# Batch 0's latent attention in one written order of instructions

## The chip, the cores and the metric

The kernel runs on one core of a Trainium2 chip. A core has five engines with a queue each: TensorE (PE) multiplies matrices and writes its products to PSUM, VectorE (DVE) works on vectors, ScalarE (ACT) computes functions such as the exponential and copies, GpSimd (POOL) does vector work on SBUF, and SyncE (SP) starts transfers. Each engine takes its instructions in the order of its own queue and waits, where it must, on semaphores of the others. The metric is the time of one execution on the device in microseconds (us), lower is better. The kernel before took 2269.19 us, the median of three runs between 2260.75 and 2271.79.

## The reference, cut to what matters

Two layers work on x, 2 batches of 1024 tokens with 128 features. Each step adds its result to x. The change is in the first step alone, a causal attention with 16 heads of 64 whose keys and values come from a latent of 32 numbers per token:

```python
q_blhd = jnp.einsum('bld,dhk->blhk', x_bld, Wq)
latent_bll = jnp.einsum('bld,dc->blc', x_bld, Wkv_down)
k_blhd = jnp.einsum('blc,chk->blhk', latent_bll, Wk_up)
v_blhd = jnp.einsum('blc,chk->blhk', latent_bll, Wv_up)
attn = jnp.einsum('bqhd,bkhd->bhqk', q_blhd, k_blhd) / jnp.sqrt(jnp.asarray(HD, dtype=x_bld.dtype))
...
attn = jax.nn.softmax(jnp.where(mask, attn, neg_inf), axis=-1)
...
x = x + _L0_attn_a_ref(_layernorm(x, axis=-1), L0_attn_a_Wq, L0_attn_a_Wkv_down, L0_attn_a_Wk_up, L0_attn_a_Wv_up, L0_attn_a_Wout)
x = x + _L0_ffn_ref(_layernorm(x, axis=-1), L0_ffn_W_fc, L0_ffn_W_proj)
x = x + _L0_attn_b_ref(_layernorm(x, axis=-1), ...)
```

After it come a feed-forward step with spiking counts, a state-space step (`attn_b`), the spiking step again, and a second layer with a linear attention, eight experts, an attention of 16 heads, and the experts again.

## The kernel before, in words

`LatentAttention` holds the first step. Wq and Wk_up are multiplied together beforehand (`wc`, scaled by 1/8), so that a head's queries live in the latent's 32 dimensions; Wv_up and Wout are multiplied to `wvo`. Tokens stand in 16 tiles of 128, four tiles make a chunk of 512, two chunks a batch. The 16 heads are C = 4 groups (`c`) of J = 4 (`j`); the four heads of a group lie in four quarters of 32 partitions.

1. `__init__` (line 135) builds constants on DVE: the mask, and the selections `ones`, `pick` and `addm`, 16 small steps of three instructions (lines 161 to 163).
2. `project` (line 168) loads five weights on ACT's queue, forms `wc` and `wvo` (16 small products each, lines 186 and 194), and then, for each of the four chunks: norm (bn_stats and bn_aggr, a square root on ACT, an inverse and four normalising instructions on DVE), four transposes, the latents in two layouts (`latT`, `lat`), and the queries of the four groups (line 221). PSUM tiles are copied out by DVE and ACT. The norm's square root and the softmax's exponential are in different function tables of ACT.
3. `row_maxima` (line 227) finds each query's largest score, exactly, before any exponential. For each tile `i` of 128 queries, each group `c` and each stretch of up to 512 keys it makes the scores of four heads on PE (line 243, with a mask product at line 252 on the last stretch) and DVE reduces them (line 261). Batch 0 takes all four heads to one PSUM tile of four banks, with two such tiles; batch 1 takes two heads to a tile of two banks, with three tiles. At the end DVE splits the negative maxima into three bf16 terms (line 272), PE transposes these and DVE copies them to `nmT`.
4. `attend` (line 283) has units (half of the queries, group, tile of 128 keys): 4 x 4 for the first half of 512 queries and 4 x 8 for the second. A unit is: scores with keys on the partitions (line 330), the maxima subtracted by a product with `addm` (line 339), the exponential on ACT (line 353), on a diagonal tile a mask on POOL (line 356), and two steps later the product with the latents (`weigh`, line 389). Denominators are, with `added`, sums over the key tiles on DVE (line 401) and one product per group (line 372); without it, one product per unit. `end` (line 407) closes a half. A unit's two PSUM tiles come from a pool of three (`a0_st`, two banks each); the outputs `a0_oT` and denominators `a0_dT` have the last two banks.

Batch 0's projections and maxima are put into order by the compiler's planner, which may move instructions ahead of others; the products are in `manual_schedule`, where every engine keeps the order in which the program writes its instructions. The helper `weave(main, side, rate)` runs `rate` steps of `side` after each step of `main`, `alternate` takes turns, `follow` puts streams one after the other, and `drain` runs a stream to its end. `first_layer` (line 1314) calls it all: project for both batches, batch 0's maxima, batch 0's products, and then, in `manual_schedule` too, the later steps of batch 0 with batch 1's maxima (rate 1.1) and products woven between them.

Of the kernel before, what the change touches and what calls it, by code (L numbers as in the profile page):

```python
# [1 line left out]

# [7 lines left out]
F32 = mybir.dt.float32  # L10
# [95 lines left out]
def drain(steps):  # L106
    for _ in steps:
        pass
# [20 lines left out]
class LatentAttention:  # L129
# [5 lines left out]
    def __init__(self, g, w, keep):  # L135
# [15 lines left out]
        nc.vector.memset(self.ones, 0.0)  # L151

        self.pick = keep.tile([P, C, P], F32, name="a0_pick")
        nc.vector.memset(self.pick, 0.0)
        for c in range(C):
            nc.vector.memset(self.ones[:, c, c::C], 1.0)
            for j in range(J):
# [8 lines left out]
                )  # L166

    def project(self, pools):
# [6 lines left out]
        with g.tc.tile_pool(name="a0_prep", bufs=1) as prep, g.tc.tile_pool(name="a0_pp", bufs=6, space=PSUM) as pp:  # L175
            w = {}
            for name in ("wkd", "wqT", "wkupT", "wvupT", "wout"):
                w[name] = g.load(name, g.dram[name], list(g.dram[name].shape), nc.scalar, prep)
            wc = prep.tile([P, 16 * LD], F32, name="a0_wc")
            wk4 = prep.tile([P, J, LD], F32, name="a0_wk4")  # L180
            for j in range(J):
                nc.gpsimd.tensor_copy(wk4[:, j, :], w["wkd"])

            psw = pp.tile([P, 512], F32, name="a0_ps")
            for h in range(16):
                nc.tensor.matmul(
                    psw[:, h * LD : (h + 1) * LD], w["wqT"][:, h, :], w["wkupT"][:, h, :], start=True, stop=True
                )

            nc.scalar.mul(wc, psw, 0.125)  # L190
            psv = pp.tile([P, C, D], F32, name="a0_ps")
            for h in range(16):
                c, j = divmod(h, J)
                nc.tensor.matmul(
                    psv[32 * j : 32 * j + 32, c, :], w["wvupT"][:, h, :], w["wout"][:, h, :], start=True, stop=True
                )
            nc.vector.tensor_copy(self.wvo, psv)

            for n in range(4):
                b, m = divmod(n, 2)  # L200
                cols = bass.ts(m, 512)
                u = prep.tile([P, 4, D], F32, name="a0_u", bufs=2)
                uT = prep.tile([P, 512], F32, name="a0_uT", bufs=2)
                ln = StagedNorm(g, g.x[:, 4 * n : 4 * n + 4, :], 4, "a0")
                ln.stats(range(4))
                ln.root()
                ln.inverse()
                ln.apply(u, range(4), nc.vector)
                pt = pp.tile([P, 4, P], F32, name="a0_ps")
                transpose4(g, pt, u)  # L210
                nc.vector.tensor_copy(uT, pt.rearrange("p a b -> p (a b)"))
                pl = pp.tile([P, 512], F32, name="a0_ps")
                nc.tensor.matmul(pl, wk4.rearrange("p a b -> p (a b)"), uT, start=True, stop=True)
                nc.scalar.copy(self.latT[b][:, cols], pl)
                plt = pp.tile([P, 4, LD], F32, name="a0_ps")
                for t in range(4):
                    nc.tensor.matmul(plt[:, t, :], uT[:, bass.ts(t, P)], w["wkd"], start=True, stop=True)
                nc.vector.tensor_copy(self.lat[b][:, 4 * m : 4 * m + 4, :], plt)
                for c in range(C):
                    pq = pp.tile([P, 512], F32, name="a0_ps")  # L220
                    nc.tensor.matmul(pq, wc[:, bass.ts(c, P)], uT, start=True, stop=True)
                    if c % 2:
                        nc.scalar.copy(self.qT[b][:, c, cols], pq)
                    else:
                        nc.vector.tensor_copy(self.qT[b][:, c, cols], pq)

    def row_maxima(self, b, seq, ps, together):


        nc, C, J = self.g.nc, self.C, self.J  # L230
        qT, latT = self.qT[b], self.latT[b]

        nm = seq.tile([P, 2, TPB, C * J], F32, name="a0_nm")
        for i in range(TPB):
            nk = (i + 1) * P
            for c in range(C):
                for half, n0 in enumerate(range(0, nk, 512)):
                    n = min(nk - n0, 512)
                    last = n0 + n == nk
                    ss = [ps.tile([P, together, 512], F32, name="a0_s", tag="a0_s") for _ in range(J // together)]  # L240
                    for j in range(J):
                        quad = slice(32 * j, 32 * j + 32)
                        nc.tensor.matmul(  # L243
                            ss[j // together][:, j % together, :n],
                            qT[quad, c, bass.ts(i, P)],
                            latT[quad, n0 : n0 + n],
                            start=True,
                            stop=not last,
                        )
                    if last:  # L250
                        for j in range(J):
                            nc.tensor.matmul(  # L252
                                ss[j // together][:, j % together, n - P : n],
# [5 lines left out]
                    for k, s in enumerate(ss):  # L259
                        h = c * J + k * together  # L260
                        nc.vector.tensor_reduce(  # L261
                            nm[:, half, i, h : h + together], s[:, :, :n], AX.X, ALU.max, negate=True
                        )
                    yield
        two = TPB // 2
        nc.vector.tensor_tensor(nm[:, 0, two:, :], nm[:, 0, two:, :], nm[:, 1, two:, :], ALU.min)
# [1252 lines left out]
```

## Time and profile before

| | |
|---|---|
| median of 3 runs | 2269.19 us |
| the profiled execution's own time | 2268.1 us |
| its span | 2266.4 us |
| PE busy over the span | 1974.6 us (87%) |
| DVE busy | 1694.8 us (75%) |
| ACT busy | 1188.3 us (52%) |
| POOL busy | 908.5 us (40%) |
| first maximum of batch 0 on DVE | 50.98 us |
| first exponential of batch 0 on ACT | 146.42 us |
| last instruction of batch 0's products on DVE | 282.8 us |

The profile is of one execution. Busy times are sums over an engine's instructions; matmuls are pipelined, so that a busy PE need not be at its peak. PE's granted clock is given as a share of full speed. In a group's line stand the source line, the engine, the operation, output and input tiles with shapes, the count, the busy time with the mean in ns, and after the second bar the idle time just before these instructions with what ended it. In a list in order of time stand start and length in us, and in square brackets the idle time before and what ended it. Tile names are cut: `a_nm` is `a0_nm`.

### The profile page before, as it was taken

The page shows a single profiled execution, that of the slowest core. Times are in us where ns is not written, and L with a number is a line of the kernel's source. Part 1 is how long each engine was busy: PE and PEld are TensorE (multiplying, and loading weights), DVE is VectorE, ACT ScalarE, POOL GpSimd, SP SyncE. Part 2 cuts the span into 40 slices and gives each one's busy share as a digit, 9 for nine tenths or more (in the row PEclk, how much of TensorE's full clock was granted, in tenths as well). Part 3 has the DMA queues.
Part 4 walks back from the last instruction along what each step waited for, and adds up shares of the span by engine and source line. Part 5 has one row for each costly group of instructions (what it writes and reads, how often), then busy time and mean ns, then how long its engine had stood idle before and what let it go on. Part 6 is the DMA issues. An engine that isn't in the chain of part 4 may idle for free. (4 is left out here: it accounts for less than half of the span.)

```text
span 2266.4 us, 36372 instructions
## 1 busy us (share of the span) xinstructions
PE 1974.6 (87%) x14832; PEld 1157.8 (51%) x14832; DVE 1694.8 (75%) x2054; ACT 1188.3 (52%) x1497; POOL 908.5 (40%) x480
## 2 busy tenths in 40 slices
PE   7679888779967558899898798988999999999999
PEld 4223343223334123344446576766777777777753
DVE  5966767897856789945323898988898899998822
ACT  1026512366624637734223675756777777777722
POOL 0013300063401020100101578887787777787720
PEclk9889988889988769999999899999999999999999
DMA  3000000395730577500000455565555555555500
GB/s 88 1 1 1 1 1 6 88 224 142 174 112 10 138 186 167 131 0 0 1 0 1 121 150 154 151 162 139 160 150 154 149 150 152 156 153 143 153 11 5
DMA packets 73798, 220.15 MB, mean 97 GB/s; under 512 B 9184, under 2 KB 19872, under 8 KB 73504
## 3 DMA queue, kind: packets, MB, share of 16 engines
q1 hardware_dynamic: 54736, 149.40, 22.0%
q0 software_dynamic: 18432, 67.12, 15.1%
q8 instruction: 116, 1.90, 0.4%
q10 hardware_dynamic: 464, 1.33, 0.3%
q14 instruction: 50, 0.41, 0.1%
HBM read 78.35 MB, written 5.24 MB: 37 GB/s over the span
## 5 line engine op out<-in xcount | busy, mean ns | idle before, releaser
L1193 POOL TENSOR_TENSOR h_a<-h_e,h_r 128x2048 f32<-128x2048 f32 x128 | 583.0, 4555 | 140.6 <-PE h_po L1199 100.2
L1159 DVE TENSOR_REDUCE h_m<-h_s 128x128 f32<-128x2048 f32 x128 | 293.2, 2291 | 70.9 <-PE h_s L1148 70.9
L1183 PE MATMUL h_pd<-h_e,ident 128*128 128x128 f32 x2048 | 264.7, 283 | 37.9 <-DMA h_e<-h_e 24.6
L1165 DVE TENSOR_TENSOR h_e<-h_s,h_m 128x2048 f32<-128x2048 f32 x128 | 292.4, 2284 | 2.3 <-DVE h_m L1159 0.6
L1168 ACT ACTIVATE h_e<-h_e 128x1024 f32<-128x1024 f32 x256 | 256.6, 1049 | 66.8 <-DVE h_e L1165 60.7
L1183 PEld LDWEIGHTS h_pd<-h_e,ident 128*128 128x128 f32 x2048 | 242.4, 194 | 80.6 <-DVE x_res L1032 47.6
L1004 ACT ACT_TABLE_LOAD x110 | 141.1, 1283 | 162.2 <-PE e_pgu L997 162.0
L356 POOL TENSOR_SCALAR_AFFINE_SELECT a_pT<-a_pT 128x256 f32<-128x256 f32 x120 | 125.9, 1072 | 223.3 <-ACT a_pT L353 137.5
L917 DVE TENSOR_TENSOR e_h<-e_sg,e_pu 128x512 f32<-128x512 f32 x128 | 87.0, 684 | 162.1 <-PE e_pu L910 136.4
L261 DVE TENSOR_REDUCE a_nm<-a_s 128x2 f32<-128x1024 f32 (+7 forms) x144 | 168.1, 1217 | 39.1 <-PE a_s L252 24.2
L912 ACT ACTIVATE e_sg<-e_pg 128x512 f32<-128x512 f32 x128 | 76.1, 596 | 191.1 <-PE e_pg L909 172.6
L1023 PEld LDWEIGHTS h_pd<-Wd,e_h 128*128 128x128 f32 x1024 | 125.1, 191 | 95.1 <-DVE e_h L1012 78.1
L353 ACT ACTIVATE a_pT<-a_st 128x1024 f32<-128x1024 f32 (+3 forms) x176 | 129.9, 792 | 72.8 <-PE a_st L339 72.0
L746 DVE TENSOR_TENSOR_SCAN s_h<-s_a,s_h 128x1024 f32<-128x1024 f32 x64 | 149.0, 2328 | 20.1 <-ACT s_a L714 15.4
L1148 PE MATMUL h_s<-h_qz,h_kT 32*128 32x512 f32 x1024 | 148.9, 651 | 17.1 <-DVE h_e L1165 12.1
L997 PE MATMUL e_pgu<-e_uT,Wg 128*128 128x256 f32 x512 | 155.0, 385 | 2.6 <-ACT h_qz L1112 2.1
L910 PE MATMUL e_pu<-e_uT,Wu 128*128 128x512 f32 x256 | 139.1, 626 | 19.5 <-DVE e_h L917 19.5
L1023 PE MATMUL h_pd<-Wd,e_h 128*128 128x128 f32 x1024 | 149.7, 288 | 6.6 <-DVE e_h L1012 3.6
L1178 POOL DMA_DIRECT2D h_e<-h_e x128 | 114.9, 898 | 100.8 <-DVE h_m L1159 48.7
L243 PE MATMUL a_s<-a_latT,a_qT 32*128 32x512 f32 (+3 forms) x768 | 117.7, 590 | 41.3 <-DVE a_nm L261 39.2
L997 PE MATMUL e_pgu<-e_uT,Wu 128*128 128x256 f32 x512 | 153.2, 381 | 0.0
L1168 ACT ACT_TABLE_LOAD x111 | 142.4, 1283 | 12.0 <-issue 7.7
(268 smaller groups left out, 3235.8 us busy)
## 6 DMA issues: line engine op xcount, KB each, us to landing
h_e<-h_e SPq DMA_DIRECT2D x128, 512.0 KB, 3.8
h_e<-h_e POOLq DMA_DIRECT2D x128, 512.0 KB, 4.5
s_a<-s_steps SPq DMA_DIRECT2D x64, 512.0 KB, 4.9
s_h<-s_steps SPq DMA_DIRECT2D x64, 512.0 KB, 6.4
s_steps<-s_gate SPq DMA_DIRECT2D x8, 256.0 KB, 3.6
Wg<-in_Wg_dram SPq DMA_DIRECT2D x8, 256.0 KB, 6.0
Wu<-in_Wu_dram SPq DMA_DIRECT2D x8, 256.0 KB, 5.9
Wd<-in_Wd_dram SPq DMA_DIRECT2D x8, 256.0 KB, 6.1
```

Of the source, the lines that this page charges most:

```text
L261: nc.vector.tensor_reduce(nm[:, half, i, h : h + together], s[:, :, :n], AX.X, ALU.max, negate=True)
L746: nc.vector.tensor_tensor_scan(h, a, h, 0.0, ALU.mult, ALU.add)
L910: nc.tensor.matmul(pu, w["Wu"][:, e, f], opened[n], start=True, stop=True)
L997: nc.tensor.matmul(pgu[:, k, :], w[name][:, e, f], uT, start=True, stop=True)
L1004: nc.scalar.activation(sg, pgu[:, 0, :], AF.Silu)
L1023: nc.tensor.matmul(po[:, t, :], h[:, bass.ts(t, P)], self.w["Wd"][:, e, fc, :], start=(k == 0), stop=(k == 1))
L1148: nc.tensor.matmul(s[:, j, :].rearrange("p (k q) -> p k q", k=K), kTs[b][quad, bass.ts(kb, P)], qzs[b][quad, :, bass.ts(qb, P)], start=Tru ...
L1159: nc.vector.tensor_reduce(m, heads.rearrange("p h q -> p q h"), AX.X, ALU.max)
L1165: nc.vector.tensor_sub(e, heads, m.unsqueeze(1).to_broadcast([P, H, P]))
L1168: nc.scalar.activation(eh, eh, AF.Exp, scale=scale)
L1183: nc.tensor.matmul(pd, g.ident, e2[:, k, :], start=(k == 0), stop=(k == 7))
L1193: nc.gpsimd.tensor_mul(a, e, r.unsqueeze(1).to_broadcast([P, H, P]))
```

## The change

Everything of batch 0's first step, the projections of both batches included, now stands in one `manual_schedule`. The methods become generators whose pieces are interleaved by hand, and one pool of three PSUM tiles of two banks (`a0_st`) serves projections, maxima and products of batch 0. Projections are made chunk by chunk; chunk 0 comes first, in turns with the query weights. Maxima are made by halves of the queries, with two heads to a PSUM tile in both batches, and each half's maxima are split and transposed on their own. The first half's maxima are woven with chunk 1 and the selections (0.6 steps to a unit); then come chunk 2 and the value weights; then the first half's products with the second half's maxima and chunk 3 (2.7 steps to a unit), and last the second half's products. The first half's denominators are now one product per unit (`added=(False, True)`). The large fills of `ones` and `pick` go to POOL, and all PSUM copies of the projections and of `nmT` to ACT.

```diff
-        nc.vector.memset(self.ones, 0.0)
...
-        nc.vector.memset(self.pick, 0.0)
+
+    def selections(self):
...
+        nc.gpsimd.memset(self.ones, 0.0)
+        nc.gpsimd.memset(self.pick, 0.0)
         for c in range(C):
...
+            yield
+
+    def open(self, pools, prep):
...
+    def query_weights(self, ps):
+        nc, w, LD = self.g.nc, self.pw, self.LD
+        psw = ps.tile([P, 2, 512], F32, name="a0_st")[:, 0, :]
+        for h in range(16):
+            nc.tensor.matmul(
+                psw[:, h * LD : (h + 1) * LD], w["wqT"][:, h, :], w["wkupT"][:, h, :], start=True, stop=True
+            )
+            if h == 7:
+                yield
+
+        nc.scalar.mul(self.wc, psw, 0.125)
+        yield
+
+    def value_weights(self, ps):
...
+        nc.scalar.copy(self.wvo, psv)
+        yield
+
+    def project(self, n, ps):
...
+        two = lambda: ps.tile([P, 2, 512], F32, name="a0_st")
...
+        ln.stats(range(4))
+        ln.root()
+        yield
+        ln.inverse()
+        ln.apply(u, range(4), nc.vector)
+        yield
+        pt = two()
+        transpose4(g, pt[:, 0, :].rearrange("p (a b) -> p a b", a=4), u)
+        nc.scalar.copy(uT, pt[:, 0, :])
+        yield
+        pl = two()
+        nc.tensor.matmul(pl[:, 0, :], self.wk4.rearrange("p a b -> p (a b)"), uT, start=True, stop=True)
+        nc.scalar.copy(self.latT[b][:, cols], pl[:, 0, :])
+        for t in range(4):
+            nc.tensor.matmul(pl[:, 1, bass.ts(t, LD)], uT[:, bass.ts(t, P)], w["wkd"], start=True, stop=True)
+        nc.scalar.copy(
+            self.lat[b][:, 4 * m : 4 * m + 4, :], pl[:, 1, 0 : 4 * LD].rearrange("p (a b) -> p a b", a=4)
+        )
+        yield
+        for c in range(0, C, 2):
+            pq = two()
+            for k in range(2):
+                nc.tensor.matmul(pq[:, k, :], self.wc[:, bass.ts(c + k, P)], uT, start=True, stop=True)
+            nc.scalar.copy(self.qT[b][:, c : c + 2, cols], pq)
+            yield
+
+    def row_maxima(self, b, half, seq, ps, tag):
...
+        nm = seq.tile([P, 2, T, C * J], F32, name="a0_nm")
+        terms = seq.tile([P, T, P], BF16, name="a0_terms")
+        nc.gpsimd.memset(terms, 0.0)
+        for i in range(T * half, T * half + T):
...
-                    ss = [ps.tile([P, together, 512], F32, name="a0_s", tag="a0_s") for _ in range(J // together)]
+                    ss = [ps.tile([P, 2, 512], F32, name=tag) for _ in range(J // 2)]
...
-        nc.vector.tensor_copy(self.nmT[b], pt.rearrange("p a b -> p (a b)"))
-        yield
...
+        nc.scalar.copy(self.nmT[b][:, bass.ts(half, 512)], pt.rearrange("p a b -> p (a b)"))
+        yield
...
-        latent.project([pool(es, "a0_batch0", 1), own])
-        with tc.tile_pool(name="a0_seq", bufs=1) as seq, tc.tile_pool(name="a0_ps_a", bufs=2, space=PSUM) as ps:
-            drain(latent.row_maxima(0, seq, ps, 4))
-        work = pool(es, "a0_work", 2)
+        latent.open([pool(es, "a0_batch0", 1), own], pool(es, "a0_prep", 1))
+        seq, work = pool(es, "a0_seq", 1), pool(es, "a0_work", 2)
         ps, ps_o = pool(es, "a0_ps_b", 3, space=PSUM), pool(es, "a0_ps_o", 1, space=PSUM)
-        with tc.manual_schedule(engines=ALL):
-            drain(latent.attend(0, work, ps, ps_o, added=True))
+        drain(alternate(latent.project(0, ps), follow(iter([None]), latent.query_weights(ps))))
+        maxima = [latent.row_maxima(0, half, seq, ps, "a0_st") for half in range(2)]
+        side = follow(latent.project(1, ps), latent.selections(), latent.project(2, ps), latent.value_weights(ps))
+        weave(islice(maxima[0], 16), side, 0.6)
+        next(maxima[0])
+        drain(islice(side, 4))
+        drain(maxima[0])
+        drain(side)
+        attend = latent.attend(0, work, ps, ps_o, added=(False, True))
+        side = follow(maxima[1], latent.project(3, ps))
+        weave(islice(attend, 15), side, 2.7)
+        drain(side)
+        drain(attend)
...
-            maxima = latent.row_maxima(1, aseq, ps, 2)
+            maxima = follow(*[latent.row_maxima(1, half, aseq, ps, "a0_s") for half in range(2)])
```

## The prediction

> **What bounds the kernel now.** I read the page first, then the busy time by stretch of the first 443 us, then groups with shapes kept apart, then the instructions in order of time around the places where the new order cuts in. The page says that the change touches little: the chain that ended last lies in the second layer, and the slices show TensorE (PE) at 6 to 9 tenths in the first fifth of the span, where this change is. So the answer comes from that fifth. In stretches (the columns are length, then busy us and instructions of PE, its weight loads, VectorE = DVE, ScalarE = ACT, GpSimd = POOL, then PE's granted clock):
>
> ```profile
> 0.00:29.00 29.00, 18.33 (x86) 13.57 (x87) 20.36 (x110) 4.13 (x8) 1.81 (x12) 1.00 0.75 172
> 29.00:50.00 21.00, 17.97 (x71) 9.54 (x69) 8.25 (x17) 5.85 (x10) 0.52 (x1) 1.00 0.00 0
> 50.00:78.00 28.00, 21.42 (x216) 10.25 (x220) 25.73 (x18) 0.00 (x0) 0.43 (x1) 0.95 0.01 1
> 78.00:142.50 64.50, 37.93 (x308) 15.16 (x300) 58.14 (x37) 0.00 (x0) 0.00 (x0) 0.87 0.00 1
> 142.50:181.20 38.70, 35.66 (x312) 13.23 (x312) 13.16 (x19) 22.56 (x34) 13.86 (x30) 0.81 0.01 1
> 181.20:283.00 101.80, 93.81 (x803) 35.37 (x801) 76.30 (x82) 60.14 (x80) 37.54 (x36) 0.98 0.01 1
> ```
>
> These are weights and chunk 0 of the projections (0 to 29), chunks 1 to 3 (to 50), maxima of the first half of batch 0's queries (to 78), of the second half (to 142.5), products of the first half up to its last unit (to 181.2), and the rest of the products. To see: DVE carries the maxima (84 of 92 us), PE the products (129 of 140) and most of the projections. Two long stretches with different bounds stand in series, which is the room that the change aims at. But DVE is busy 20 us in the first 29, where PE waits for weights until 9.75, so some of its work is already covered there.
>
> The prices of a maximum, four heads to an instruction now (first two lines), two heads in batch 1, which the changed batch 0 will use too (last four):
>
> ```profile
> L261 DVE TENSOR_REDUCE a_nm<-a_s 128x4 f32<-128x2048 f32 x24 | 53.9, 2283 | 5.1 <-PE a_s L243 4.6
> L261 DVE TENSOR_REDUCE a_nm<-a_s 128x4 f32<-128x1536 f32 x8 | 13.8, 1750 | 0.3 <-PE a_s L252 0.2
> ...
> L261 DVE TENSOR_REDUCE a_nm<-a_s 128x2 f32<-128x1024 f32 x48 | 56.4, 1217 | 14.1 <-PE a_s L243 9.4 <-PE a_s L252 4.5
> L261 DVE TENSOR_REDUCE a_nm<-a_s 128x2 f32<-128x768 f32 x16 | 14.5, 948 | 4.1 <-PE a_s L252 4.0
> L261 DVE TENSOR_REDUCE a_nm<-a_s 128x2 f32<-128x512 f32 x16 | 10.3, 685 | 7.9 <-PE a_s L252 7.9
> L261 DVE TENSOR_REDUCE a_nm<-a_s 128x2 f32<-128x256 f32 x16 | 6.0, 414 | 5.0 <-PE a_s L252 5.0
> ```
>
> And how three PSUM tiles of two heads behave in batch 1, in order of time:
>
> ```profile
> 428.01 1.13 PE L243 MATMUL a_s<-a_latT,a_qT 32*128 32x512 f32 x4
> 428.21 2.35 DVE L261 TENSOR_REDUCE a_nm<-a_s 128x2 f32<-128x1024 f32 x2
> 429.49 1.13 PE L243 MATMUL a_s<-a_latT,a_qT 32*128 32x512 f32 x4 [0.35 <-DVE a_nm L261]
> 430.55 0.40 PE L252 MATMUL a_s<-a_mask,a_identb 128*128 128x128 bf16 x4
> 430.87 2.36 DVE L261 TENSOR_REDUCE a_nm<-a_s 128x2 f32<-128x1024 f32 x2 [0.31 <-PE a_s L252]
> ```
>
> To see: where the second tile of a unit waits for a buffer, its two pairs of heads take 1.13 us each, against 1.14 for all four together in an undisturbed unit; and DVE stands 0.31 us per masked unit. PE goes on only as far as the rotation of three tiles lets it.
>
> **The change part by part.** I follow the new order stage by stage and compare when it reaches the last unit of the first half's products, at 181.2 now.
>
> Chunk 0. PE starts at 9.75 as now, since the five weight loads keep their place on ACT's queue and the loads on SP's are not moved. At the cold prices of now: query weights 7.0, transposes 1.1, latents 2.05 + 1.75, queries 5.3: done at 27, first maximum at 28, instead of 51. Selections and value weights have left this stretch, and so have chunks 1 to 3.
>
> First half's maxima with chunk 1 and three quarters of the selections. DVE: 8 x (0.414 + 0.685 + 0.948 + 1.217) = 26.1; chunk 1's norm 3.1 (four each of 0.285, 0.159 and 0.28, and an inverse); the selections cost 8.4 now (16 x 0.215, 0.171, 0.141), so 6.3. Sum 35.5. Selections were hidden under the weights' arrival; that cover is gone, and behind them in DVE's queue stand maxima, for which PE's tiles wait. Gaps: 0.31 x 16 less the five places that inserted DVE work fills, 3.4; chunk 1's insertions on PE (transposes 0.6, latents 2.1, two query pairs 1.84 each) with the next unit's 1.0 to 1.4, less the 1 to 2 us of maxima that DVE has in hand, open about 4. Together 43: to 71.
>
> Between the halves the order is serial. On DVE: three-term split 1.4, last selections 2.1, chunk 2's statistics 1.8, the root's round trip 0.5, inverse and normalising 1.3: 7.1. Only then PE's transposes of chunk 2, queued ahead of everything else, can go: PE stands 7 us. Then chunk 2 on PE and value weights with DVE empty. Chunk 0 took 18.5 to 29.2 cold, so 10.7; a warm chunk took 35.8 to 42.0, so 6.2; with maxima's transposes and value weights 13 cold, 8 warm. What a stop does to the clock is here:
>
> ```profile
> 135.00:141.00 6.00, 0.90 (x11) 0.50 (x8) 5.34 (x8) 0.00 (x0) 0.00 (x0) 0.62 0.00 1
> 141.00:147.00 6.00, 4.55 (x24) 1.86 (x21) 0.69 (x1) 1.86 (x2) 0.00 (x0) 0.50 0.00 0
> 147.00:153.00 6.00, 5.06 (x28) 1.97 (x28) 0.00 (x0) 3.96 (x6) 2.44 (x6) 0.50 0.00 0
> 153.00:159.00 6.00, 6.00 (x52) 2.19 (x50) 4.11 (x6) 2.04 (x4) 1.96 (x3) 0.67 0.01 3
> ```
>
> Five us without work cost the clock until about 158, so I take 13: 71 + 7 + 13 = 91 for the first product. [...]
>
> First half's products with the second half's maxima. DVE has 32 x 1.217 + 26.1 = 65 us over 32 units, woven 2.7 to a product step, so 12 steps of 5.4. What decides is how long DVE is empty per step. Take PE at the end of a step's last maximum: DVE has that unit's two tiles before it, on average 2.0 us. PE then writes the step's scores: the first pair at once (0.7 on average over widths 512, 384, 256, 128), the second when the first of the two tiles is reduced (1.1 to 1.8), bias terms 0.3 to 2.1. Behind these in PE's queue stand weighing and, since this half no longer sums on DVE, denominators: both have the rows 1.07, 0.85, 0.64, 0.42, mean 0.745, so 1.5, to 3.6. Next unit's scores 1.1: DVE gets work at 4.65, having been empty 2.65. Step: 5.4 + 2.65 = 8.05, twelve steps 97, to 188. Bounds: empty 0 (65, if PE always runs ahead) and 3.15 with 0.5 more for masks (103).
>
> Last three steps: split 1.4, three products of 3.7, 2.9 and 2.2 on PE, a warm chunk 3 of 6.2, and about 2 us in which PE waits for the norm, with its root between exponentials: 17.5, to 205.5. That root needs two ACT_TABLE_LOADs that are not there now, 1283 ns each by the page's row, 2.6 together, inside those 2 us. [...]
>
> The rest is the order of now, 101.8 us: end at 307.3 against 283.0, **+24**. Rest of the edits: copies moved from DVE to ACT (0.66 to 0.69 each, queries at 1.03 for 1024 columns) cost nothing where ACT is busy under a quarter; behind the products, 22.6 of 38.7, they add at most 2. POOL's fills (about 1 us) stand behind nothing. DVE's sums that go (13 us) lie beside PE. Batch 1's maxima in halves add five short operations of 0.25 and take a 0.69 copy to ACT, and halve the 4.2 us tail at 438.6: between -2 and +2, taken as 0. Profiled run 2268.1 (span 2266.4), 1 us under the median 2269.19: **2292**; its own range, stages at their bounds, 2276 to 2303.
>
> **The rivals.** (1) Not slower: DVE's empty time per step in the woven stretch goes. For: PE busy there is only 3.6 + 2.7 x 1.1 = 6.6 of 8.05. Against: one order per engine, three tiles. Fully gone it is worth 12 x 2.65 = 32: 2260; with a warm chunk 2 and no gaps in the first stretch 15 less. It decides from 0.65 us down, where 2.0 x 12 equals the 24. Chance 0.17 (2245 to 2274). (2) The clock falls at the stop and stays down for 17 us, as from 141 to 158, into the products: half of about 15 us, and again whenever PE starves: 2304 or more. For: the rows above. Against: PE is busier than that in the woven stretch. 0.14. (3) The change moves nothing on balance: front as fast as now (78) and the gaps half as long: 2268 less 0 to plus 10. 0.09. (4) Forecast as worked out, 0.60.
>
> **How the numbers follow.** Half a percent (11 us) is about what can be told from no change. Slower: most of the forecast's 0.60 (0.56) and rival 2, 0.70. Same: forecast's low end 0.04, rival 3, and 0.06 of rival 1, 0.19. Faster: 0.11, rival 1's rest. Range: 2257 leaves out 0.10 below, 2307 0.10 above.
>
> **What would show it.** First maximum near 28; a PE stop of 5 to 8 us near 71 to 78 with the clock at 0.5 behind it; first exponential near 91; in the woven stretch a period of about 8 us with DVE empty 2 to 3 us under "PE a_st"; its last unit near 205. Wrong if that period is 6 us or less, or if the first exponential comes before 80.

## The result, and the profile after

The kernel with the change took **2306.51 us** (median of four runs, 2304.51 to 2308.63) against 2270.49 us before (four runs, 2260.75 to 2272.13): 1.0161 times as long, with a 95% interval of 1.0141 to 1.018. The direction was forecast, the size was not: +36 us where +24 was predicted. The time lies above the 2276 to 2303 that the forecast gave as its own range.

The profiled execution took 2305.7 us (span 2304.0). The whole loss lies in batch 0's first step: its last addition to x (the DVE line `x_res<-x_res,a_st`) starts at 318.20 us, before at 282.07, so 36.1 later, and what follows lasts nearly as long as before (1985.8 us from there to the end of the span, against 1984.3). In this text "the end of the step" is always that instruction. It is a cleaner measure than the total, because the remaining 1980 us vary from one profile to the next, between 1979 and 1996 in the runs below.

Busy time by stretch of the kernel after, cut where the stages of the prediction meet (columns: length, then busy us and count of PE, its weight loads, DVE, ACT, POOL, then PE's granted clock, DMA share, GB/s):

```profile
0.00:28.00 28.00, 18.72 (x66) 12.81 (x66) 3.40 (x17) 5.29 (x8) 3.27 (x16) 1.00 0.78 177
28.00:76.90 48.90, 41.02 (x204) 19.26 (x202) 32.86 (x85) 4.11 (x7) 0.00 (x0) 0.69 0.00 1
76.90:96.00 19.10, 12.12 (x50) 6.31 (x54) 5.72 (x31) 3.73 (x7) 0.00 (x0) 0.54 0.00 0
96.00:201.20 105.20, 94.72 (x656) 38.09 (x644) 61.65 (x65) 18.92 (x29) 10.08 (x25) 0.85 0.00 1
201.20:217.40 16.20, 13.12 (x101) 5.74 (x98) 4.22 (x19) 10.72 (x15) 2.48 (x6) 1.00 0.00 1
217.40:318.90 101.50, 94.26 (x813) 36.05 (x812) 73.73 (x76) 60.92 (x81) 38.42 (x36) 0.97 0.01 1
```

The first row is chunk 0, and DVE is busy for 3.4 us of it where it had 20.4 of its first 29 before: the cover that the selections had is empty now. The second row is the first half's maxima. The clock, third from the end of each row, is what the prediction did not have: 0.69, 0.54 and 0.85 in three stretches in a row, where the same work before ran at 1.00 (projections) and 0.87 to 0.95 (maxima). PE is busy for 41.0 of the 48.9 us of the second row, which holds chunk 1 too; with four heads to a tile and no chunk beside them it was 21.4 of 28.0. One reading of the clock is not to be trusted: the first row says 1.00, but chunk 0's first latent product takes 2.07 us there, and the same product 1.13 us in the kernel before at 30.48 us, so chunk 0 ran cold now as it did before.

Within the second row the clock is low twice before PE stops, and PE is busy both times:

```profile
33.00:48.00 15.00, 14.32 (x70) 8.30 (x67) 6.79 (x15) 1.44 (x3) 0.00 (x0) 0.50 0.00 1
64.00:73.00 9.00, 8.66 (x28) 2.95 (x28) 7.08 (x18) 0.00 (x0) 0.00 (x0) 0.50 0.00 0
```

The stop between the halves, PE in order of time (start, length, instructions, and in brackets the idle time before and its releaser):

```profile
72.05 0.61 PE L276 MATMUL a_st<-a_mask,a_identb 128*128 128x128 bf16 x4
82.89 1.15 PE L115 MATMUL a_st<-ident,a_u 128*128 128x128 f32 x4 [10.24 <-DVE a_u L74]
...
89.26 6.21 PE L245 MATMUL a_st<-a_uT,a_wc 128*128 128x512 f32 x8
95.39 1.08 PE L208 MATMUL a_st<-wout,wvupT 64*32 64x128 f32 x32
96.40 1.29 PE L353 MATMUL a_st<-a_qT,a_latT 32*128 32x512 f32 x8
```

PE has written its last maximum's scores at 72.65 and next works at 82.89, when DVE has finished the last maximum, four selections, the three-term split, four more selections and chunk 2's norm. The queries' products of chunk 2 then take 6.21 us at half clock, where the same four took 3.68 at full clock in the kernel before. (An f32 product of this kind stands as two instructions in the trace: four products are x8.) The first product of the next stage starts at 96.40.

ACT in order of time, the exponentials that start every fourth step of the woven stretch, and the two table loads around chunk 3's root:

```profile
98.44 1.94 ACT L376 ACTIVATE a_pT<-a_st 128x1024 f32<-128x1024 f32 x2
...
130.76 1.94 ACT L376 ACTIVATE a_pT<-a_st 128x1024 f32<-128x1024 f32 x2 [7.27 <-PE a_st L362]
...
163.49 1.94 ACT L376 ACTIVATE a_pT<-a_st 128x1024 f32<-128x1024 f32 x2 [10.01 <-PE a_st L362]
...
201.32 1.94 ACT L376 ACTIVATE a_pT<-a_st 128x1024 f32<-128x1024 f32 x2 [9.48 <-PE a_st L362]
...
204.05 1.28 ACT L67 ACT_TABLE_LOAD   x1
...
205.66 1.28 ACT L376 ACT_TABLE_LOAD   x1
```

Twelve steps take 102.9 us, 8.6 each. The same stretch, cut at these three exponentials, by busy time:

```profile
98.40:130.80 32.40, 27.87 (x181) 13.05 (x179) 15.90 (x20) 5.26 (x10) 3.67 (x9) 0.68 0.00 1
130.80:163.50 32.70, 29.05 (x222) 11.70 (x220) 21.27 (x22) 5.64 (x10) 3.20 (x8) 0.95 0.01 1
163.50:201.30 37.80, 35.51 (x226) 12.10 (x224) 24.58 (x23) 5.66 (x9) 3.20 (x8) 0.91 0.00 1
```

DVE is empty for 16.5, 11.4 and 13.2 us, so 4.1, 2.9 and 3.3 a step. In the four steps that ran at a clock of 0.95 it was 2.9, and the forecast had 2.65. DVE's own work a step is 4.0, 5.3 and 6.1 us, since the maxima get wider, where the forecast had its mean, 5.4, throughout.

### The profile page after: what moved, and what is told of

It reads as the page before. It is cut to its first block, busy times and chain, and to the rows that moved or that the text cites. A ratio compares the mean times of both kernels' runs of the same rounds, so it can differ in the third digit from the quotient of the medians.

```text
span 2304.0 us, 36570 instructions
## 1 busy us (share of the span) xinstructions
PE 2024.7 (88%) x14928; PEld 1181.0 (51%) x14928; DVE 1673.5 (73%) x2067; ACT 1199.8 (52%) x1512; POOL 905.8 (39%) x484
## 5 line engine op out<-in xcount | busy, mean ns | idle before, releaser
L1216 POOL TENSOR_TENSOR h_a<-h_e,h_r 128x2048 f32<-128x2048 f32 x128 | 581.5, 4543 | 141.1 <-PE h_po L1222 101.8
L1188 DVE TENSOR_TENSOR h_e<-h_s,h_m 128x2048 f32<-128x2048 f32 x128 | 292.4, 2284 | 2.3 <-DVE h_m L1182 0.6
L376 ACT ACTIVATE a_pT<-a_st 128x1024 f32<-128x1024 f32 (+3 forms) x184 | 137.6, 801 | 153.1 <-PE a_st L362 152.8
L285 DVE TENSOR_REDUCE a_nm<-a_st 128x2 f32<-128x1024 f32 (+3 forms) x96 | 86.5, 951 | 91.4 <-PE a_st L276 53.4
L1222 PE MATMUL h_po<-h_a,h_vz 128*32 128x128 f32 x4096 | 140.1, 278 | 0.0
```

The lines of the kernel that those rows point to most:

```text
L1188: nc.vector.tensor_sub(e, heads, m.unsqueeze(1).to_broadcast([P, H, P]))
L1216: nc.gpsimd.tensor_mul(a, e, r.unsqueeze(1).to_broadcast([P, H, P]))
L1222: nc.tensor.matmul(po[32 * j : 32 * j + 32, :], vz[:, kb * J + j, k].rearrange("p a d -> p (a d)"), a[:, 4 * j + k, :], start=(kb == 0 and ...
```

## The experiments

Three explanations were open. (A) The order itself: the stop and DVE's empty time per step, as forecast. (B) The clock: with this order PE runs at half speed where the forecast had it warm. (C) Two heads to a tile instead of four cost more than batch 1's rows showed. The first four experiments change one place of the order each, in the changed kernel. Ratios are against executions of the kernel before that were run beside each experiment (medians 2270.26 to 2273.05 us).

**Chunk 2 out of the stop.** Chunk 2 goes behind the second half's maxima, so that between the halves only the split, the transposes, the last selections and the value weights are left.

```diff
-        side = follow(latent.project(1, ps), latent.selections(), latent.project(2, ps), latent.value_weights(ps))
+        side = follow(latent.project(1, ps), latent.selections(), latent.value_weights(ps))
...
-        drain(islice(side, 4))
-        drain(maxima[0])
         drain(side)
+        drain(maxima[0])
...
-        side = follow(maxima[1], latent.project(3, ps))
-        weave(islice(attend, 15), side, 2.7)
+        side = follow(maxima[1], latent.project(2, ps), latent.project(3, ps))
+        weave(islice(attend, 15), side, 3.1)
```

> Chunk 2 no longer stands between the halves; it follows the second half's maxima in the woven stretch (3.1 steps to a product step). Order theory (DVE and PE stand in each other's way in one written order; clock secondary): the front ends 12 to 14 us earlier (first exponential near 85 instead of 98), the woven stretch takes a warm chunk more, 6 us, so 6 to 8 us less in all, 2299. Clock theory (the 12 us beyond my forecast are the clock that fell in this stop): the first steps of the woven stretch run warm as well, 8 us more, so 14 to 16 less, 2291. If chunk 2 costs as much in its new place: 2306.

Measured: 2306.01 us (2304.54 to 2311.38), 1.015 times before (1.0134 to 1.0165), so no gain on the changed kernel. The first exponential came at 81.60, 16.8 us earlier than with the change, and the second half's maxima were split 23 us earlier, but the end of the step was at 315.47, only 2.7 earlier. By stretch:

```profile
80.00:178.00 98.00, 86.17 (x596) 35.19 (x588) 61.76 (x66) 16.93 (x25) 9.31 (x23) 0.89 0.00 1
178.00:215.00 37.00, 28.37 (x176) 11.93 (x180) 7.03 (x33) 18.37 (x26) 3.20 (x8) 0.82 0.00 1
```

The second row is where the gain went: chunks 2 and 3 now stand one after the other at the end, with two roots and four table loads among the last exponentials. That stretch lasts 37 us, with the change 16.2. The stop was moved, not removed.

**No weaving.** The second half's maxima and chunk 3 are run to their end before the first product.

```diff
         side = follow(maxima[1], latent.project(3, ps))
-        weave(islice(attend, 15), side, 2.7)
         drain(side)
         drain(attend)
```

> The second half's maxima and chunk 3 run before the first product; nothing is woven into the products. The woven stretch of the changed kernel took 121 us (96 to 217). Order theory: 65 us of maxima with 0.3 of gap a unit make 75, split and transposes 3, chunk 3 with its norm 8, fifteen product steps 39 to 43: 125 to 129, so 2310 to 2315: weaving was worth under 8 us of the 41 that it laid beside the maxima. If weaving works as meant, its loss costs 25 us or more: over 2331. Clock theory: between, as the clock falls again before the products: 2315 to 2320.

Measured: 2322.76 us (2322.27 to 2328.06), 1.0224 (1.0209 to 1.024), 16 us slower than the change. Weaving was expected to be worth less than 8 us; it is worth twice that. The second half's maxima by stretch, with nothing beside them:

```profile
98.00:140.00 42.00, 36.23 (x174) 20.13 (x174) 30.02 (x36) 0.00 (x0) 0.00 (x0) 0.54 0.00 1
140.00:182.00 42.00, 39.47 (x140) 15.82 (x136) 32.01 (x30) 0.00 (x0) 0.00 (x0) 0.50 0.00 1
```

They take 84 us, where four heads to a tile took 61 (78 to 138.9), and the clock is at 0.50 to 0.54 throughout, with PE busy for 39.5 of the last 42 us. This was the first sign that B and C are the same thing: maxima of two heads to a tile, alone on PE, run at half clock. With the change's products between them it is at 0.85.

**Half steps.** A yield between a unit's scores and its weighing, so that maxima come in twice as often: two smaller gaps instead of one.

```diff
                 held[step] = h.exponentials(c, kb)
+                if h.half == 0 and b == 0 and step < 15:
+                    yield
...
-        weave(islice(attend, 15), side, 2.7)
+        weave(islice(attend, 30), side, 1.35)
```

> A product step of the first half is cut in two, scores and exponentials in the one, weighing and denominators in the other, with 1.35 steps of maxima after each. Order theory: PE's block between two maxima falls from 3.6 us to 2.1 and 1.5, DVE's empty time per full step from 2.65 to about 1.8, over twelve steps 10 us less: 2296. Clock theory: the first steps stay cold, no more than 3 us less: 2303 or more.

Measured: 2308.21 us (2303.98 to 2314.34), 1.0157 (1.0134 to 1.018): no change of the total. The woven stretch did shrink:

```profile
96.00:196.70 100.70, 88.83 (x675) 37.45 (x677) 62.48 (x66) 19.86 (x30) 10.08 (x25) 0.89 0.00 1
196.70:218.00 21.30, 18.22 (x118) 8.10 (x114) 3.99 (x18) 11.60 (x17) 2.48 (x6) 0.76 0.00 1
```

From the first exponential to the second half's split it is 96.0 us instead of 103.1, 7 of the 10 that were expected, so DVE's gap behind a product block is real. But the stretch began 2 us later, and the next one, chunk 3 among the last units, took 4 to 5 us more at a clock of 0.76 where the change had 1.00. The end of the step was at 317.5.

**Idle products in the stop.** Eight products whose results nobody reads keep PE busy while DVE works. Nothing of the computation is left out in this or any other experiment.

```diff
         next(maxima[0])
+        idle = ps_o.tile([P, 512], F32, name="a0_oT")
+        for _ in range(8):
+            g.nc.tensor.matmul(idle, g.ident, latent.latT[0][:, 0:512], start=True, stop=True)
         drain(islice(side, 4))
```

> Eight products of 128x512 (f32, results unused) are added on PE in the stop between the halves, where PE stood from 72.7 to 82.9; nothing else changes. Clock theory: chunk 2 runs at the warm 6.2 instead of 10.7 and the first steps of the woven stretch warm, 8 to 12 us less: 2296. Order theory: the clock is a part of the price of the stop, 4 to 6 less: 2301. If the idle products do not hold the clock up, 0 to 4 more, as cold they last 14 us: 2306 to 2311.

Measured: 2296.28 us (2293.73 to 2300.98), 1.0099 (1.0082 to 1.0116): adding useless work made the changed kernel 10 us faster. PE in order of time, and the stretches of the stop and the weaving:

```profile
74.01 8.28 PE L1365 MATMUL a_oT<-a_latT,ident 128*128 128x512 f32 x16
84.46 1.01 PE L115 MATMUL a_st<-ident,a_u 128*128 128x128 f32 x4 [2.17 <-DVE a_u L74]
```

```profile
78.40:96.00 17.60, 14.24 (x56) 6.79 (x58) 5.77 (x32) 3.65 (x7) 0.00 (x0) 0.81 0.00 0
96.00:197.20 101.20, 90.23 (x661) 35.55 (x656) 61.88 (x65) 19.17 (x30) 10.07 (x25) 0.92 0.00 1
```

The idle time on PE in the stop falls from 10.24 to 2.17 us, and the clock rises from 0.54 to 0.81 in the stop and from 0.85 to 0.92 in the woven stretch, which ends 4 us earlier. Cut every four steps, as above:

```profile
98.50:126.30 27.80, 22.77 (x178) 10.40 (x176) 15.90 (x20) 5.20 (x9) 3.67 (x9) 0.88 0.00 1
126.30:159.20 32.90, 29.25 (x224) 11.60 (x223) 21.27 (x22) 5.71 (x10) 3.20 (x8) 0.95 0.01 1
159.20:197.00 37.80, 35.50 (x226) 12.08 (x224) 24.59 (x23) 5.64 (x9) 3.20 (x8) 0.91 0.00 1
```

The gain is in the first four steps alone, 27.8 us for 32.3; the other eight last as long as with the change. The profile is of the slowest of the four executions, and its end of the step is 4.3 us earlier than with the change; the median gains 10. B is part of the loss.

**Selections early.** The 16 selections, hidden before under the weights' arrival, run right behind chunk 0's norm, where DVE has 20 us without work.

```diff
-        drain(alternate(latent.project(0, ps), follow(iter([None]), latent.query_weights(ps))))
+        drain(
+            alternate(
+                latent.project(0, ps),
+                follow(iter([None]), latent.query_weights(ps)),
+                follow(iter([None, None]), latent.selections()),
+            )
+        )
...
-        side = follow(latent.project(1, ps), latent.selections(), latent.project(2, ps), latent.value_weights(ps))
+        side = follow(latent.project(1, ps), iter([None] * 4), latent.project(2, ps), latent.value_weights(ps))
```

> The selections run on DVE behind chunk 0's norm, where DVE stood from 7.9 to 28 us; their places among the first half's maxima stay empty. Order theory: 8.4 us of DVE work leave its queue, 6 of them in the first half's maxima and 2 in the stop; PE is cold there and limits part of it, so 5 to 8 us less, 2300. Clock theory: what goes is filled by cold PE work, only the 2 us in the stop remain, and as DVE then stands more the clock falls earlier: 2304 to 2308.

Measured: 2289.91 us (2288.85 to 2293.59), 1.0084 (1.0062 to 1.0107), by its median the fastest version of the change: 16.6 us under it, where 5 to 8 were expected. By stretch:

```profile
0.00:28.00 28.00, 18.60 (x62) 12.62 (x63) 10.79 (x68) 4.96 (x8) 3.27 (x16) 1.00 0.82 177
28.00:71.70 43.70, 38.78 (x210) 18.47 (x206) 27.52 (x45) 4.45 (x7) 0.00 (x0) 0.76 0.00 1
71.70:88.00 16.30, 11.32 (x60) 6.11 (x60) 3.91 (x18) 4.17 (x7) 0.00 (x0) 0.60 0.00 0
88.00:188.40 100.40, 89.43 (x644) 35.54 (x644) 61.87 (x65) 18.59 (x30) 10.08 (x25) 0.92 0.00 1
```

DVE works 7.4 us more in the first row and the first maximum comes at 28.32 instead of 27.99. The split comes at 71.73 instead of 76.88 and the first exponential at 90.0 instead of 98.44: 8.4 us, as much as the selections cost on DVE (8.4). The woven stretch then gains another 4.5 us, at a clock of 0.92 for 0.85, again all in its first four steps (27.8). Together these make nearly the 13.1 by which the end of the step is earlier; the rest of the 16.6 lies behind the step, within what the profiles vary. So the selections cost their own time, which the forecast had in its sum, and clock besides.

**The kernel before with two heads to a tile.** Only C, alone: the maxima of batch 0 take two heads to a tile with three tiles, as in the change, and nothing else is changed.

```diff
-        with tc.tile_pool(name="a0_seq", bufs=1) as seq, tc.tile_pool(name="a0_ps_a", bufs=2, space=PSUM) as ps:
-            drain(latent.row_maxima(0, seq, ps, 4))
+        with tc.tile_pool(name="a0_seq", bufs=1) as seq, tc.tile_pool(name="a0_ps_a", bufs=3, space=PSUM) as ps:
+            drain(latent.row_maxima(0, seq, ps, 2))
```

> The kernel before with one part of the change: batch 0's maxima with two heads to an instruction and three PSUM tiles of two banks; its order stays. 48 units cost 0.151 us more each on DVE (7 us), and 0.3 of wait on PE a masked unit, 10 in all, against 8 us of gaps now: 6 to 12 us more than before, 2277 to 2283. If PE keeps DVE fed as it does with four heads: 7 more, 2278. If the clock falls in the maxima, as the gaps are many: up to 20 more.

Measured: 2315.72 us (2311.51 to 2318.47), 1.0194 (1.0171 to 1.0217). This one edit costs at least as much as the whole change. Part of that is the planner, which put two heads, their two masks, the next two heads in PE's queue, where it had four heads and four masks; so the same with four tiles,

```diff
-tc.tile_pool(name="a0_ps_a", bufs=2, space=PSUM) as ps:
-            drain(latent.row_maxima(0, seq, ps, 4))
+tc.tile_pool(name="a0_ps_a", bufs=4, space=PSUM) as ps:
+            drain(latent.row_maxima(0, seq, ps, 2))
```

> As the run with three tiles, but with four, which take the same eight banks as before's two tiles of four heads. If the rotation of three tiles is what starves DVE, the fourth brings back its gaps: 7 us more than before, 2278, and 3 to 6 less than with three. If the size of the instruction alone counts, both runs agree.

which gave no steady time, and so no ratio (2303.33, 2307.95, 2317.01, and once 2268.19, the time of the kernel before); and the same with three tiles in the written order, which is what the change has:

```diff
         with tc.tile_pool(name="a0_seq", bufs=1) as seq, tc.tile_pool(name="a0_ps_a", bufs=3, space=PSUM) as ps:
-            drain(latent.row_maxima(0, seq, ps, 2))
+            with tc.manual_schedule(engines=ALL):
+                drain(latent.row_maxima(0, seq, ps, 2))
```

> The kernel before with two heads to an instruction and three PSUM tiles for batch 0's maxima, in manual_schedule, so that PE's order in them is that of before (four heads, then four mask products); with the planner it had gone over to pairs. Order theory: pairs were most of the 43 us of that run; here 7 us of longer DVE work and 3 to 7 of waits remain: 2281 to 2287. Clock theory: the wait for a buffer parts the four heads all the same and the clock falls to 0.5 for the whole of the maxima, as it did without weaving: 84 us for the second half instead of 61, 2300 to 2315.

Measured: 2306.09 us (2288.03 to 2312.34), 1.0143 (1.0094 to 1.0193). The maxima last from 51.76 to 178.46, 127 us where four heads to a tile took 88, and the end of the step is at 320.41, 38 us after that of the kernel before. By stretch, first the kernel before, then this one:

```profile
51.00:95.00 44.00, 31.01 (x296) 14.60 (x292) 38.32 (x27) 0.00 (x0) 0.00 (x0) 0.88 0.00 1
95.00:139.00 44.00, 26.33 (x208) 9.26 (x204) 43.37 (x24) 0.00 (x0) 0.00 (x0) 0.93 0.00 1
```

```profile
78.00:100.00 22.00, 20.92 (x86) 9.13 (x80) 14.81 (x14) 0.00 (x0) 0.00 (x0) 0.50 0.00 1
...
140.00:160.00 20.00, 20.00 (x72) 8.41 (x72) 14.73 (x14) 0.00 (x0) 0.00 (x0) 0.50 0.00 1
```

With four heads to a tile PE is busy for 57 of 88 us and its clock is near 0.9. With two it is busy for 20.00 of 20.00 us and the clock is 0.50. Is the clock the cause of the 38 us, or do two heads cost PE more by themselves, so that it only looks so?

**The same with an idle product behind each unit.** One product of full 128 rows, 512 columns, results unread, behind each of the 48 units' scores. If PE's work were the bound, this could only cost time.

```diff
+                    if idle is not None:
+                        nc.tensor.matmul(idle, self.g.ident, latT[:, 0:512], start=True, stop=True)
                     for k, s in enumerate(ss):
```

> The kernel before with two heads to a tile in its own order, as in the run that took 127 us for the maxima at a clock of 0.5, with one idle product of 128x512 behind each of the 48 units. Clock theory: full-array products hold the clock and the maxima fall to 90 to 100 us although PE has 41 us more to do: 2275 to 2285. Order theory (PE is the bound because a wait for a buffer parts the four heads, whatever the clock): the idle products come on top, 127 us or more: 2306 to 2325.

Measured: 2283.63 us (2278.49 to 2291.70, ten runs), 1.0053 (1.0034 to 1.0073). The maxima take 106 us instead of 127, and the end of the step is at 300.88, 19.5 us earlier. By stretch of this kernel:

```profile
51.00:100.00 49.00, 48.79 (x316) 20.48 (x317) 35.66 (x46) 0.16 (x1) 0.69 (x1) 1.00 0.00 1
100.00:150.00 50.00, 50.00 (x265) 18.92 (x265) 43.72 (x45) 0.00 (x0) 0.00 (x0) 1.00 0.00 1
```

And the groups of the 512 wide score products, the same 96 in the three kernels (x192 instructions; busy us and mean ns behind the bar): four heads to a tile,

```profile
L243 PE MATMUL a_s<-a_latT,a_qT 32*128 32x512 f32 x192 | 29.8, 694 | 23.2 <-DVE a_nm L261 23.2
```

two heads to a tile,

```profile
L243 PE MATMUL a_s<-a_latT,a_qT 32*128 32x512 f32 x192 | 67.6, 1135 | 0.0
L261 DVE TENSOR_REDUCE a_nm<-a_s 128x2 f32<-128x1024 f32 x48 | 56.2, 1219 | 22.4 <-PE a_s L243 11.3 <-PE a_s L252 11.1
```

and two heads with idle products.

```profile
L263 DVE TENSOR_REDUCE a_nm<-a_s 128x2 f32<-128x1024 f32 x48 | 56.2, 1219 | 11.3 <-PE a_s L243 8.6 <-PE a_s L252 2.7
L260 PE MATMUL a_idle<-a_latT,ident 128*128 128x512 f32 x96 | 52.5, 628 | 0.0
L243 PE MATMUL a_s<-a_latT,a_qT 32*128 32x512 f32 x192 | 30.8, 640 | 0.0
```

The scores fall from 67.6 to 30.8 us, 52.5 us of useless products come on top, and DVE still waits half as long before its widest maxima (11.3 for 22.4). At a clock of 1.00 the scores of two heads to a tile take about what those of four take at 0.88 and 0.93 (30.8 and 29.8). So the clock, and not the count of products, made PE the bound: B is how C costs. What two heads cost without idle products at full clock no run shows; it is at most the 18 us that are left (106 against 88). Nor does any run give the changed kernel its four heads to a tile back.

**Idle products in the change's first half of maxima.** One behind each of the 16 units, beside the eight in the stop:

```diff
-        weave(islice(maxima[0], 16), side, 0.6)
+        idle = ps_o.tile([P, 512], F32, name="a0_oT")
+
+        def idle_product():
+            g.nc.tensor.matmul(idle, g.ident, latent.latT[0][:, 0:512], start=True, stop=True)
+
+        def with_idle(steps):
+            for _ in steps:
+                idle_product()
+                yield
+
+        weave(with_idle(islice(maxima[0], 16)), side, 0.6)
         next(maxima[0])
+        for _ in range(8):
+            idle_product()
```

> One idle product of 128x512 behind each unit of the first half's maxima, beside the eight in the stop, which alone gave 2296. Clock theory: full-array products hold the clock through the 49 us of the first half's maxima (it was 0.69 there), which then end 6 to 10 us earlier: 2288. Order theory: sixteen products of 0.86 us stand in PE's queue before the next scores and DVE waits for them, 0 to 6 more: 2296 to 2302.

Measured: 2300.08 us (2293.86 to 2304.60), 1.0121 (1.0089 to 1.0152). The clock is 1.00 from 28 to 75, the split comes at 73.94 (78.44 with the idle products in the stop alone) and the end of the step at 307.48, 10.7 earlier than with the change and close to the 307.3 of the forecast. The total doesn't follow: the rest of the kernel took 1995.4 us in this profile, of the slowest of the four executions, 10 more than with the change.

**Selections early and idle products.** Four in the stop, and, in another run, one behind each unit of the first half's maxima.

```diff
         next(maxima[0])
+        idle = ps_o.tile([P, 512], F32, name="a0_oT")
+        for _ in range(4):
+            g.nc.tensor.matmul(idle, g.ident, latent.latT[0][:, 0:512], start=True, stop=True)
```

> Selections early and four products of 128x512 (results unused) in the stop. Alone the two gave 16.6 and 10.2 us. If the gains are of different places they add, less the 2 us by which the stop is shorter: 2281 to 2284. If both work through the clock at the begin of the woven stretch, which was up after the early selections already: 2287 to 2290.

```diff
-        weave(islice(maxima[0], 16), side, 0.6)
+        weave(with_idle(islice(maxima[0], 16)), side, 0.6)
```

> Selections early, and an idle product of 128x512 behind each unit of the first half's maxima. With early selections alone these maxima took 28 to 72 us at a clock of 0.76. Clock theory: at full clock they end 4 to 7 us earlier, near 66, and the first step ends near 299 instead of 305: 2284. Order theory: DVE waits for the idle products, nothing gained: 2290.

Measured: 2292.40 (2291.02 to 2295.86), 1.0098 (1.0075 to 1.0121), nothing beyond the early selections; its end of the step is at 304.84, theirs at 305.14. And 2294.06 (2290.21 to 2297.58), 1.0096 (1.0068 to 1.0125). In the second the stage did what was expected: the split at 67.64, the first exponential at 83.80, the end of the step at 299.27 (expected near 299), with

```profile
28.00:69.00 41.00, 37.48 (x232) 16.52 (x232) 27.91 (x49) 3.76 (x6) 0.00 (x0) 1.00 0.00 1
```

at full clock with 16 products more. But the rest of the kernel took 1995.5 us again, 13 more than with early selections alone. Why it does so in both kernels with idle products among the maxima stays open; what the program has behind this step is the same, and there is one profile of each. Without it this version would be near 2284, an estimate (the profiled execution's 2297.4 less 13), still slower than before.

**Two that gave nothing.** DVE's sums of the first half's denominators put back, and five idle products in the kernel before while its maxima are split:

```diff
-        attend = latent.attend(0, work, ps, ps_o, added=(False, True))
+        attend = latent.attend(0, work, ps, ps_o, added=(True, True))
```

> The first half's denominators are sums on DVE again (added for both halves). PE's block between two maxima falls by 0.475 us on average, DVE takes 1.2 us of sums a step into time in which it stood. Order theory: 12 x 0.475, 4 to 6 us less: 2301. If the sums stand before the next maxima on DVE and delay PE's buffers: 5 to 10 more: 2314.

```diff
+        if together == 4:
+            idle = ps.tile([P, together, 512], F32, name="a0_s", tag="a0_s")
+            for _ in range(5):
+                nc.tensor.matmul(idle[:, 0, :], self.g.ident, latT[:, 0:512], start=True, stop=True)
         two = TPB // 2
```

> The kernel before with five products of 128x512 (f32, results unused) on PE while DVE splits the last maxima (PE stood from 135.7 to 140.8). Clock theory: the clock, which was at 0.5 from 136 to 158 there, stays up, and the first products run at the warm 34 instead of 39 us: 4 to 8 us less than before, 2263 to 2267. If the clock falls in spite of them: 0 to 1 more.

Measured: 2311.75 (2298.63 to 2318.35), 1.0174 (1.0133 to 1.0214), with the end of the step 3.5 us later than with the change (2.4 of them stand already at the first half's split, ahead of the edit), so the denominators on PE were not the loss. And 2278.05 (2262.43 to 2286.35, twelve runs), 1.0018 (0.9998 to 1.0037): in the kernel before the clock fell at 147 all the same (1.00 up to there, 0.50 from 150 to 153), and nothing was gained. No version in this study beat the kernel before.

## Why the prediction was wrong

Stage by stage, in the prediction's own terms, in us:

| stage | forecast | measured | clock |
|---|---|---|---|
| chunk 0, to the first maximum | 28 | 28.0 | cold, by its products |
| first half's maxima, chunk 1, selections ("Together 43") | 43 | 48.9 | 0.69 |
| stop and chunk 2, to the first product ("7" and "13 cold") | 20 | 19.5 | 0.54 |
| woven stretch ("twelve steps 97") | 97 | 104.8 | 0.85 |
| last three steps, to the last unit | 17.5 | 16.2 | 1.00 |
| the rest of the step | 101.8 | 101.5 | 0.97 |
| end of the stage | 307.3 | 318.9 | |

The mechanism was right in its parts: DVE's serial stop, the cold chunk behind it, and DVE standing empty behind each product block. The first maximum came at 27.99. DVE's serial work from the split to the end of the norm took 6.6 us (forecast 7.1), and the 13 for the cold chunk and the value weights was 13.5. The period of a step is 8.1 and 8.2 us in the first two thirds of the woven stretch, where 8.05 was forecast. In the first third that is luck: DVE has 4.0 us of work there for the 5.4 forecast, and stands empty for 4.1 instead of 2.65. The table loads came where they were said to, 1.28 us each. The terms written for the last three steps add up to 18.4, not to the 17.5 of the forecast; 16.2 was measured. The root and the next exponential follow their table loads within 0.02 us (at 205.35 and 206.96).

**The terms that failed are two, the "43" and the "97", by 5.9 and 7.8 us.** Both were summed at warm prices, and the larger part of each is the clock. The forecast counted a cold clock only inside the stop, "as from 141 to 158", and let it be warm before and after. Measured, it is at 0.50 from 33 to 48 and from 64 on, before PE has stopped at all, and at 0.64 from 96 to 120, after the stop.

For the "43": with an idle product behind each unit the clock is 1.00, and the split comes 45.6 us after the first maximum instead of 48.9 (50.3 in the run that has idle products in the stop alone). So 3.3 to 4.7 of the 5.9 us are the clock, with the idle products paid.

For the "97": 4.5 of the 7.8 us are the clock. The first four steps take 32.3 us at a clock of 0.68, and 27.8 at 0.88 in all five runs with idle products or early selections in the changed kernel. Of the remaining 3.3, 2.0 pass between the first product and the first exponential, which the forecast left out, and 1.3 are the twelve steps themselves (27.8, 32.7 and 37.8 make 98.3, for 97). The last two thirds are equally long in all these runs, so what is over in them is not shown to be the clock.

Behind that is one step of the working: the price of two heads to a tile was read from batch 1, "three PSUM tiles of two heads behave in batch 1", at 1.217 us a tile on DVE and 0.31 of waiting a unit. There PE's queue holds full-array products of the later steps among the scores, and the clock was 1.00 where these lines stand (0.86 on average from 283 to 442.8, the stretch of batch 1's maxima). In batch 0 the scores stand nearly alone. The run that changes this alone, in the kernel before, shows its price: +38 us at the end of the step, about as much as the whole change (+36.1), and the run with idle products shows that at least 19.5 of these are the clock. The change's weaving gains some of it back: without it another 16 us would be lost.

Rival 2, that the clock falls at the stop and stays down into the products, was given 2304 or more and 0.14, and the result lies there. It is right for the first four steps: idle products in the stop return these 4.5 us (4.3 are left at the end of the step, and the median gains 10). The cold time in the first half's maxima, before the stop, it does not have. Rival 1 (DVE's empty time goes) is excluded by the steps, rival 3 (gaps half as long) too.

"Selections were hidden under the weights' arrival; that cover is gone" was right and was worth more than its 8.4: moved back under the weights they save 13.1 at the end of the step and 16.6 of the median.

## What to carry to other kernels

A price read from a group's row holds at the clock of that row (here 1135 ns for a 512 wide score instruction at 0.50, 640 at 1.00): before it is carried to another stage, read the granted clock there and what else stands in PE's queue. Where PE is nearly always busy and still at half clock, adding a full-array product per unit is a cheap test of whether its time is work or clock (here 127 us of maxima became 106). And work that lies under a load's arrival is free only there (here the selections, 8.4 us of DVE, 13.1 at the end of the step): when the order around it is rewritten, put it back under that load first, and only then ask what the rest of the order is worth.

## What the runs showed of the hardware

The granted clock did not follow how busy PE was. In the kernel before with scores of two heads at a time, each in 32 of the 128 rows, and in the planner's order, it stayed at 0.50 for 112 us (75 to 187), though the profile has PE busy for 107.85 of them. The products' lengths agree: its 192 score instructions 512 wide took 1130 ns each on average, and 694 in the kernel before. By stretch:

```profile
75.00:99.00 24.00, 24.00 (x68) 6.96 (x66) 12.17 (x12) 0.00 (x0) 0.00 (x0) 0.50 0.00 1
...
147.00:171.00 24.00, 24.00 (x85) 8.07 (x86) 18.31 (x18) 0.00 (x0) 0.00 (x0) 0.50 0.00 1
```

In the written order it was 0.50 as well, with PE busy for 20.00 of 20.00 us (140 to 160). Four heads at a time had it at 0.88 and 0.93, with PE busy for 57.3 of 88 us, and with one product over all 128 rows per unit it was 1.00 from 51 to 150, with PE busy for 98.79 of 99. Chunk 1's latent product over all 128 rows did not bring it back: at 39.97 in the kernel after, within the stretch at 0.50, it took 2.02 us, and 1.13 at 30.48 in the kernel before. Which property of the products makes the difference no run isolates. Nor was the clock the same in every execution of a kernel: with four tiles of two heads one of four took 2268 us at a mean clock of 0.944, the others 2303 to 2317 at 0.915 to 0.920.
